# A recommender with two recurrent layers: the order of work between the first layer and the second

## The chip, the cores and the metric

The kernel runs on one core of one Trainium2 chip. The metric is the time on the device of one execution, in microseconds (us); lower is better. Three runs of the kernel before took 2012.16, 2012.26 and 2012.96 us, median 2012.26.

## What is computed

The reference handles 1024 users, each with a history of 100 items of 128 features, and gives one score for each. A GRU runs over the history and gives `keys`; a small attention network scores every key against the item; the weighted sum of the keys is `pooled`. A second recurrent layer (AUGRU) runs over the same keys with an update gate that is scaled by a number for each step and user, taken from `pooled.T`. Its state at the end of the user's own history goes into a last small network.

```python
def gru_step(h, x_t):
    gi = x_t @ gru_Wih.T + gru_bih
    gh = h @ gru_Whh.T + gru_bhh
    ...
    h_new = (1.0 - z) * n + z * h
...
score = _mlp(feat, [(att_W0, att_b0), (att_W1, att_b1), (att_W2, att_b2)], jax.nn.relu)
attn = jax.nn.softmax(score, axis=1)[..., 0]
pooled = jnp.einsum('bt,btd->bd', attn, keys)
att_seq = pooled.T[:T]

def augru_step(h, inp):
    x_t, a_t = inp
    ...
    u = a_t[:, None] * u
    h_new = (1.0 - u) * h + u * h_hat
```

The second layer can't begin before `pooled` is complete, since the number of its step t is feature t of `pooled`. The softmax over the history has to be complete for that.

## The kernel before, in words

Data lie with features on the 128 partitions and users along the free axis, in two halves of 512 users (`Half`, `HB`). Instructions stand in each engine's queue in the order in which the program issues them (`tc.manual_schedule`), and each engine has one queue. The program has two parts.

**The GRU part** (`gru_phase`, L201) loops over 100 steps and both halves; a step is packed matmuls of 32 output columns each. Beside it run the attention network (`attend`, L714), the softmax in blocks (`softmax`, L790), the weighted sums on POOL and DVE (`Half.pool`, L630) and the store of every four keys to memory (`Half.store`, L620: 1 MB for each half, on SP's DMA queue). After the last step, L956 to L1062, come the tail of the attention network, the last block of the softmax and the rest of the sums. In that tail:

- `half.store((T - 1) // G)` at L1021 puts the last keys of both halves in SP's queue.
- `gather_early(n)` (L887) issues the next n gathers of key rows (`load_row`, L183, the DMA at L190) from POOL. They bring keys 4 to 11 of half 0, sorted by length of history, 16 rows in all; 13 are issued in the GRU part, the rest at L1464.
- POOL forms the first 16 columns of each 32-column block of the sums for half 0, DVE for half 1 (L1043 to L1045). L1047 stores the first 16 features: half 1 by SP's queue, half 0 by ACT's.
- `half.pool(T, nc.vector, rest)` at L1054 leaves DVE with the other columns, reading the softmax weights from PSUM. The multiply is L652, the add L653.

**The branch** (L1533). A number worked out from the lengths, `over`, is loaded into a register of each engine. It selects one of three copies of the AUGRU part, written out for other widths: each step handles only the users whose history is still running, sorted by length. The copy for the usual widths is `augru(0)`; with these inputs it is the one that runs. In the program's text it stands last, in the Else part of the outer test.

**The AUGRU part** (`augru_phase`, L1064) gathers the stored weights in sorted order (`gather_weights`, L1094, four DMAs from POOL at L155 for each half), then issues the remaining row gathers, then opens the three gates of step 1 of both halves with the part of the matmuls that needs keys alone (`open_gates`, L1182, matmul at L1187). `EARLY_BANKS` and `LATE_BANKS` say which PSUM banks these six take; the banks were used by the GRU part. `first_state` (L1119) turns column 0 of the gathered weights into a row with four matmuls against an identity (L1111) and multiplies it into the state of step 0, on DVE (L1122, L1123). Then come the steps:

- `half_step(t, i)` (L1202) closes the gates with the state (`close_gate`, L1189, matmul at L1191), lets ACT apply the sigmoids and DVE do the rest, and opens the gates of the half's next step. Both halves alternate.
- `load_key(t, i)` (L1156) brings the key of step t. For keys 0 to 3 it transposes four 128x128 tiles on TensorE (L1170) into the one bank of the pool `pa` and ACT copies it out (L1171); for later keys DVE transposes 32x32 blocks. Keys 2 and 3 are loaded within steps 1 and 2.
- `first_weights`, `store_weights` and `load_att` bring the numbers of step 1, and those of later steps through memory.
- From step `one` on both halves go together (`whole_step`, L1273).
- `predict(0, last=True)` (L1324) computes the last scores; DVE adds them to the earlier ones in `all_y` (L1414), which `earlier_results` loads at L1438, and SP stores the 1024 scores (L1415), the last instruction of the copy.

After the branch all engines meet in a closing barrier.

Of the kernel before, what the change touches and what calls it, by code (L numbers as in the profile page):

```python
# [9 lines left out]
F32 = mybir.dt.float32  # L10
# [9 lines left out]
P = 128  # L20
B = 1024
T = 100
HB = 512
NH = B // HB
# [3 lines left out]
R = 32  # L28
KH = HB // R
# [22 lines left out]
G = 4  # L52
# [3 lines left out]
FIRST = [sum(READ[:q]) for q in range(len(READ))]  # L56
# [23 lines left out]
BQ = B // (P // R)  # L80
# [4 lines left out]
def kernel(ctx: ExitStack, tc: tile.TileContext, a: dict, out: bass.AP):  # L85
# [26 lines left out]
    nc = tc.nc  # L112
# [25 lines left out]
    item = const.tile([P, B], F32, name="item")  # L138
    hist = const.tile([P, B], F32, name="hist")
    pooled = const.tile([P, NK, R], F32, name="pooled")  # L140
    idx = const.tile([P, GH, NH * 3], I32, name="idx")
    idx_k = const.tile([P, KH, NH], I32, name="idx_k")
    used_s = const.tile([P, NH, GH, SOON], U8, name="used_s")
# [2 lines left out]
    h3 = [h_all[:, i, :] for i in range(NH)]  # L146
# [4 lines left out]
    later = {}  # L151
# [49 lines left out]
    def gru_phase(pools):  # L201
# [32 lines left out]
        wp = pools.enter_context(tc.tile_pool(name="wp", bufs=2))  # L234
# [7 lines left out]
        for _ in range(2):  # L242
            p = pa.tile([P, HB], F32, tag="a", name="pd")
# [465 lines left out]
        halves = [Half(i) for i in range(NH)]  # L709
# [177 lines left out]
        def gather_early(n):  # L887
            for _ in range(n):
                next(more_early)
# [3 lines left out]
        for s in range(T):  # L893
            last = s == T - 1
            n, due = divmod(s - again, 4)
            n, i = divmod(n, NH)
# [120 lines left out]
        some(6, 7)  # L1017
        for half in halves:
            key(1, half)
        for half in halves:  # L1020
            half.store((T - 1) // G)  # L1021
        stage(2)
        exponents()
        for half in halves:
            gates = (item[:, half.cols], s_bs[NH * ((soft["j"] - 1) % 2) + half.i])
            later["gates", half.i] = gates
            for to, (n, f) in zip(gates, (("u", AF.Sigmoid), ("h", AF.Tanh))):
                if half.i:
                    p = banks["f"].pop(0)
                else:  # L1030
                    p = pa.tile([P, HB], F32, tag="a", name=f"p{n}")
                nc.tensor.matmul(
                    p,
                    lhsT=later["w" + n][:, 1, :],
                    rhs=later["key", 0, half.i],
                    start=True,
                    stop=True,
# [5 lines left out]
        halves[0].product(soon)  # L1043
        halves[0].pool(T, nc.gpsimd, soon)
        halves[1].pool(T, nc.vector, soon)  # L1045
        gather_early(3)
        for half, eng in zip(reversed(halves), (nc.sync, nc.scalar)):  # L1047
            eng.dma_start(
                out=pooled_d[0][half.cols, :].rearrange("(k r) c -> r k c", r=R),
                in_=pooled[:R, half.ks, soon],  # L1050
            )
        for half in reversed(halves):
            half.todo = late[half.i]
            half.pool(T, nc.vector, rest)  # L1054
            t = blocked(s_bs[NH * (soft["j"] % 2) + half.i])
            nc.vector.tensor_mul(t, later["used"][:, half.ks, :], pooled[:, half.ks, :])
            to = pooled_d[1][half.cols, :].rearrange("(k r) f -> r k f", r=R)
            later["att", half.i] = [(to[:, :, : R - SOON], t[:R, :, rest])]
            later["att", half.i] += [
                (to[:, :, p * R - SOON : (p + 1) * R - SOON], t[p * R : (p + 1) * R])  # L1060
                for p in range(1, P // R)
            ]  # L1062

    def augru_phase(pools, widths, alive):  # L1064
# [4 lines left out]
        wp = pools.enter_context(tc.tile_pool(name="wp3", bufs=3))  # L1069
# [11 lines left out]
        wr, wu, wh = later["wr"], later["wu"], later["wh"]  # L1081
# [5 lines left out]
        def bank(name, n=None):  # L1087

            if n is None:
                n = ring.pop(0)  # L1090
                ring.append(n)
            return ps[n].tile([P, HB], F32, tag="g", name=name)
# [26 lines left out]
        def first_state(i, p):  # L1119
            weight_row(0, i, p)  # L1120
            u, h = gates[i]
            nc.vector.tensor_mul(p, p, u)  # L1122
            nc.vector.tensor_mul(h3[i], p, h)  # L1123
            r = sorted_rows[i][:, :, 1:SOON]
            nc.vector.tensor_mul(r, r, used_s[:, i, :, 1:])
# [30 lines left out]
        def load_key(t, i):  # L1156

            q = max(j for j, first in enumerate(FIRST) if first <= t)
            w, m, r = widths[t], t - FIRST[q], rows[q, i]
            if t >= one and i:  # L1160
                k = keys.pop((t, 0))
            else:
                k = qp.tile([P, HB], F32, name="k3")
            keys[t, i] = k
            if t >= one:
                k = k[:, ts(i, P)]
            if q < WHOLE:
                p = pa.tile([P, HB], F32, tag="a", name="pk3")
                for g in range(-(-w // P)):
                    nc.tensor.transpose(p[:, ts(g, P)], r[:, g, ts(m, P)], ident)  # L1170
                nc.scalar.copy(k[:, :w], p[:, :w])  # L1171
            else:
                w, n = -(-w // R), KH // len(r)
                for j, part in enumerate(r):
                    u = min(w - j * n, n)
                    if u > 0:
                        nc.vector.transpose(
                            k.rearrange("p (k r) -> p k r", r=R)[:, j * n : j * n + u, :],
                            part[:, :u, ts(m, R)],
                        )  # L1180
# [21 lines left out]
        def half_step(t, i):  # L1202


            w, h = widths[t], h3[i][:, : widths[t]]
            before, after = ((t - 1, 1), (t, 1)) if i == 0 else ((t, 0), (t + 1, 0))
            if before in resets:
                open_state(*before)
            pr = close_gate(t, i, "pr", wr, h)
            pu = close_gate(t, i, "pu", wu, h)  # L1210
            nc.scalar.activation(pr, pr, AF.Sigmoid, bias=later["br"])
            nc.scalar.activation(pu, pu, AF.Sigmoid, bias=later["bu"])
            state = states.pop(1 - i, None)
            if state is not None:
                nc.vector.tensor_mul(state[0], state[0], state[1])  # L1215
            r = wp.tile([P, HB], F32, name="r3")[:, :w]
            nc.vector.tensor_mul(r, h, pr)
            if state is not None:
                nc.vector.tensor_sub(state[3], state[0], state[2])
            if t == 1:  # L1220
                first_weights(i, spare)
                load_key(2, i)
            nc.vector.tensor_mul(pu, pu, att.pop((t, i))[:, :w])
            rest = wp.tile([P, HB], F32, name="rest")[:, :w]

            nc.vector.scalar_tensor_tensor(  # L1226
                out=rest, in0=pu, scalar=1.0, in1=h, op0=ALU.subtract, op1=ALU.mult
            )
            later["pace"] = rest[:, 0:1]
            resets[t, i] = r, pu, rest  # L1230
            if after[0] < min(T, one) and (*after, "pr") not in opened:
                open_gates(*after)
            elif after[0] == one < T:
                open_both(one, "pr", "pu", "ph")
            if t == 1 and i:
                store_weights(1, spare)
                load_key(3, 0)
            elif t == 1:
                open_state(1, 0)
                store_weights(0, pa.tile([P, HB], F32, tag="a", name="pw"))  # L1240
                first_state(1, spare)
            elif t == 2 and i == 0:
                load_key(3, 1)
            if t + 2 < T:
                load_att(t + 2, i)

            if t == FIRST[1] - 1:
                load_key(t + 1, i)
            if FIRST[1] - 2 < t < T - 2:
                load_key(t + 2, i)  # L1250
# [73 lines left out]
        def predict(g, last=False):  # L1324
# [80 lines left out]
            for q in range(P // R):  # L1405
# [4 lines left out]
                    start=True,  # L1410
                    stop=True,
                )
            all_y = later["all_y"]
            nc.vector.tensor_add(all_y, p, all_y)  # L1414
            nc.sync.dma_start(  # L1415
                out=out.rearrange("(q c) -> q c", c=BQ),
                in_=all_y.rearrange("(q r) c -> q r c", r=R)[:, 0, :],
            )

        def last_places():  # L1420
            own = sp.tile([P, 1], F32, name="own3", bufs=1)
# [12 lines left out]
                later["places"].append(row)  # L1434

        def earlier_results():
            later["all_y"] = wp.tile([P, BQ], F32, tag="att_t", name="all_y", bufs=2)
            nc.sync.dma_start(  # L1438
                out=later["all_y"],
                in_=early_d.rearrange("(q c) o -> q (o c)", c=BQ)  # L1440
                .unsqueeze(1)
                .to_broadcast([P // R, R, BQ]),
            )
# [17 lines left out]
        gates = [later["gates", i] for i in range(NH)]  # L1461
        keys.update({(1, i): later["key", 1, i] for i in range(NH)})
        sorted_rows = [gather_weights(i) for i in range(NH)]
        for k in range(13, KH):  # L1464
            load_row(1, 0, k)
        open_gates(1, 1, EARLY_BANKS)
        open_gates(1, 0, LATE_BANKS)
        spare = bank("spare", EARLY_BANKS[-1])
        first_state(0, pa.tile([P, HB], F32, tag="a", name="first"))
        ahead = load_rows(1, 1, widths[FIRST[1]], kp)  # L1470
        due = spread_over(-(-widths[FIRST[1]] // R), NH * (FIRST[1] - 2))
# [57 lines left out]
    def augru(n):  # L1529
        with ExitStack() as pools, tc.manual_schedule():  # L1530
            augru_phase(pools, WIDTHS[n], ALIVE[n])

    over = nc.values_load(over_d, min_val=0, max_val=len(LINES))  # L1533
    with tc.If(over > 0) as many:
        with tc.If(over < 2) as fits:
            augru(1)
        with fits.Else():
            augru(2)
    with many.Else():
        augru(0)  # L1540


# [64 lines left out]
```

## Time and profile before

| what | value |
|---|---|
| median of 3 runs | 2012.26 us |
| the profiled execution | 2012.06 us |
| its span in the profile | 2010.3 us |
| TensorE (PE) busy | 1987.7 us, 99% |
| VectorE (DVE) busy | 1673.9 us, 83% |
| GpSimd (POOL) busy | 1273.8 us, 63% |
| ScalarE (ACT) busy | 936.0 us, 47% |
| last GRU-part matmul ends | 1405.51 us |
| first AUGRU-part matmul starts | 1410.66 us |
| last store issued (L1415) | 2007.65 us |
| DMA traffic | 204.88 MB, mean 102 GB/s |

The profile is of one execution. Its times count from the start of the span; the execution's own time has some 1.8 us more around the span. Lines such as L652 are lines of the kernel before. A line of the timeline gives start, length, engine, line, operation, the tiles written and read, and in brackets how long the engine had been idle and who ended that. A line of the chain of work that ended last gives start, length and engine or DMA. PEld is TensorE's weight load. SPq and ACTq are the DMA issues of SP and ACT. In a table of stretches each engine has its busy time in us and its number of instructions; then come the granted clock of TensorE as a share of full speed, the busy share of the DMA engines and GB/s.

### The profile page before, as it was taken

The numbers are of one execution on the slowest core, as the hardware profiler recorded it, in microseconds if no ns is written. First come the engines' busy times: TensorE is split into PE (matmuls) and PEld (weight loads), VectorE is DVE, ScalarE is ACT, GpSimd is POOL, SyncE is SP. The second block draws the span as 40 slices with busy tenths as digits, with TensorE's granted clock in tenths as the row PEclk, the third lists the DMA queues.
The fourth block names the chain that finished last, engine by engine and source line by source line (L and its number), as shares of the span: only waits on it lengthen the run. The fifth ranks groups of instructions, "written<-read, shape, count | busy, mean of one in ns | idle before, by whom it ended". The sixth has DMA issues, their size and how long they took to land.

```text
span 2010.3 us, 40989 instructions
## 1 busy us (share of the span) xinstructions
PE 1987.7 (99%) x15348; PEld 1198.2 (60%) x15348; DVE 1673.9 (83%) x3033; ACT 936.0 (47%) x1681; POOL 1273.8 (63%) x1325
## 2 busy tenths in 40 slices
PE   9999999999999999999999999999899999999998
PEld 2346666666555555555555555545444556678997
DVE  7888999887978887888878888998577778888985
ACT  4445454454444454444444454455243444455553
POOL 0333939669796959495887868898674454445331
PEclk9999999999999999999999999999899999999998
DMA  4443333323334434333333333332543333343331
GB/s 124 98 117 92 107 104 102 94 82 104 115 113 103 118 108 123 115 109 105 106 101 99 107 98 101 107 95 76 138 126 103 96 110 97 94 103 95 85 80 28
DMA packets 243152, 204.88 MB, mean 102 GB/s; under 512 B 60582, under 2 KB 205966, under 8 KB 242942
## 3 DMA queue, kind: packets, MB, share of 16 engines
q1 hardware_dynamic: 229646, 169.55, 30.4%
q0 software_dynamic: 12480, 32.05, 5.8%
q8 instruction: 123, 2.02, 0.4%
q14 instruction: 87, 0.71, 0.1%
q10 hardware_dynamic: 816, 0.56, 0.1%
HBM read 146.03 MB, written 54.41 MB: 100 GB/s over the span
## 4 chain that ended last, share of the span: by engine, by line
PE 96%; DVE 1%; DMA 1%; issue 0%; ACT 0%; POOL 0%; SPq 0%; DVEq 0%; POOLq 0%; ACTq 0%
PE ps L547 51%; PE pm L723 18%; PE ph L1191 4%; PE pr L1191 4%; PE pu L1191 4%; PE pu L1187 4%; PE ph L1187 4%; PE pr L1187 4%; DMA rows<-keys_d,idx_k 1%; PE last L690 1%; PE pr L1269 0%; DMA item<-in_item 0%; PE ph L1269 0%; PE p L1389 0%; DVE pu L1215 0%
## 5 line engine op out<-in xcount | busy, mean ns | idle before, releaser
L547 PE MATMUL ps<-x,wih 128*32 128x512 f32 x4800 | 712.5, 593 | 0.0
L547 PE MATMUL ps<-hn,whh 128*32 128x512 f32 x4752 | 705.9, 592 | 1.3 <-ACT hn L595 1.3
L547 PEld LDWEIGHTS ps<-x,wih 128*32 128x32 f32 x4800 | 301.9, 110 | 225.7 <-issue 39.7
L547 PEld LDWEIGHTS ps<-hn,whh 128*32 128x32 f32 x4752 | 299.5, 110 | 222.5 <-issue 35.5
L559 ACT ACTIVATE r<-ps,brz 128x512 f32<-128x512 f32 x200 | 137.5, 688 | 382.6 <-PE ps L547 382.4
L532 POOL TENSOR_TENSOR xm<-x,m 128x512 f32<-128x512 f32 x200 | 234.9, 1175 | 68.2 <-DMA m<-mask_d 67.9
L533 POOL TENSOR_TENSOR hist<-hist,xm 128x512 f32<-128x512 f32 x200 | 258.2, 1291 | 15.7
L190 POOL DMA_INDIRECT rows<-keys_d,idx_k x218 | 212.5, 975 | 82.2 <-POOL rows L189 45.9
L653 POOL TENSOR_TENSOR pooled<-pooled,kw 128x512 f32<-128x512 f32 (+1 forms) x190 | 243.7, 1283 | 14.9
L652 POOL TENSOR_TENSOR kw<-kt,e 128x512 f32<-128x512 f32 (+1 forms) x190 | 205.6, 1082 | 67.9 <-DVE e L841 67.9
L723 PE MATMUL pm<-hn,wk 128*32 128x512 f32 x1200 | 245.5, 592 | 0.6 <-issue 0.6
L723 PE MATMUL pm<-kq,wkq 128*32 128x512 f32 x1200 | 245.5, 592 | 0.0
L578 ACT ACTIVATE ps<-ps,bih 128x512 f32<-128x512 f32 x200 | 132.4, 662 | 224.8 <-DVE ps L577 223.8
L567 DVE SCALAR_TENSOR_TENSOR u<-ps,bhh,r 128x512 f32<-128x512 f32 x198 | 147.5, 745 | 70.6 <-PE ps L547 68.1
L1199 ACT ACTIVATE c<-ph,bh 128x510 f32<-128x510 f32 (+57 forms) x174 | 88.1, 506 | 251.0 <-PE ph L1191 203.3
L723 PE MATMUL pm<-mv,w 128*32 128x512 f32 (+1 forms) x808 | 194.9, 592 | 0.0
L582 DVE TENSOR_TENSOR d<-hn,ps 128x512 f32<-128x512 f32 x198 | 136.1, 687 | 35.9 <-ACT ps L578 35.2
L583 DVE TENSOR_TENSOR d<-ps,d 128x512 f32<-128x512 f32 x200 | 138.4, 692 | 29.1 <-ACT ps L579 13.3
L595 ACT COPY hn<-ps 128x512 f32<-128x512 f32 x200 | 116.4, 582 | 94.3 <-DVE kq L589 92.6
L189 POOL COPY rows<-rest 128x1 f32<-128x1 f32 x202 | 38.0, 188 | 192.6 <-DVE rest L1226 186.5
L577 DVE TENSOR_TENSOR ps<-ps,u 128x512 f32<-128x512 f32 x200 | 140.0, 700 | 20.8
L584 DVE TENSOR_TENSOR ps<-ps,d 128x512 f32<-128x512 f32 x200 | 139.9, 699 | 6.8
(255 smaller groups left out, 3141.0 us busy)
## 6 DMA issues: line engine op xcount, KB each, us to landing
x<-in_hist_x SPq DMA_DIRECT2D x210, 256.0 KB
keys_d<-kt SPq DMA_DIRECT2D x48, 1024.0 KB
m<-mask_d SPq DMA_DIRECT2D x200, 128.0 KB
rows<-keys_d,idx_k POOLq DMA_INDIRECT x218
s_b<-mv SPq DMA_DIRECT2D x200, 8.0 KB
keys_d<-kt SPq DMA_DIRECT2D x32, 64.0 KB
mask_i<-in_mask SPq DMA_DIRECT2D x8, 200.0 KB
part_d<-part SPq DMA_DIRECT2D x2, 400.0 KB
```

The costliest lines, as they stand in the source:

```text
L190: nc.gpsimd.indirect_dma_start(out=r[:, at, :], out_offset=None, in_=keys_d[q], in_offset=bass.IndirectOffsetOnAxis(ap=idx_k[:, k, i : i + ...
L532: nc.gpsimd.tensor_mul(d, x, m)
L533: nc.gpsimd.tensor_add(acc, acc, d)
L547: nc.tensor.matmul(p[ts(q, R), :], lhsT=w[:, g, ts(q, R)], rhs=v, start=(j == 0), stop=(j == len(parts) - 1),)
L567: nc.vector.scalar_tensor_tensor(out=u, in0=ph, scalar=bhh[:, 2:3], in1=r, op0=ALU.add, op1=ALU.mult,)
L577: nc.vector.tensor_add(pi, pi, u)
L584: nc.vector.tensor_add(pi, pi, d)
L652: eng.tensor_mul(d, k, w)
L653: eng.tensor_add(acc, acc, d)
L723: nc.tensor.matmul(p[i][s, :], lhsT=w[:, s], rhs=v, start=start, stop=stop)
L1187: nc.tensor.matmul(p, lhsT=m[:, 1, :], rhs=k, start=True, stop=False)
L1191: nc.tensor.matmul(p, lhsT=m[:, 0, :], rhs=v, start=False, stop=True)
```

## The change

- The test of the branch is turned round: `augru(0)` is now the first body, and the other two stand behind it.
- The store of the scores moves from the end of the copies to behind the branch. `all_y` is no tile of the AUGRU part any more but lies in the memory of `pooled`.
- `load_key` for steps 2 and 3, both halves, moves from steps 1 and 2 to between the opening matmuls and `first_state`. Three matmuls into the bank `spare` are added behind them; nothing reads their result.
- The store of the last keys moves behind the store of the pooled sums.
- One row gather moves from the GRU part to behind the gathers of the weights.

```diff
@@ tile_rec_kernel
     pooled = const.tile([P, NK, R], F32, name="pooled")
+    all_y = pooled.rearrange("p k r -> p (k r)")[:, :BQ]
@@ gru_phase, after the last step
         for half in halves:
             key(1, half)
-        for half in halves:
-            half.store((T - 1) // G)
         stage(2)
...
         halves[0].pool(T, nc.gpsimd, soon)
         halves[1].pool(T, nc.vector, soon)
-        gather_early(3)
+        gather_early(2)
         for half, eng in zip(reversed(halves), (nc.sync, nc.scalar)):
             eng.dma_start(
                 out=pooled_d[0][half.cols, :].rearrange("(k r) c -> r k c", r=R),
                 in_=pooled[:R, half.ks, soon],
             )
+        for half in halves:
+            half.store((T - 1) // G)
@@ half_step
             if t == 1:
                 first_weights(i, spare)
-                load_key(2, i)
...
             if t == 1 and i:
                 store_weights(1, spare)
-                load_key(3, 0)
             elif t == 1:
                 open_state(1, 0)
                 store_weights(0, pa.tile([P, HB], F32, tag="a", name="pw"))
                 first_state(1, spare)
-            elif t == 2 and i == 0:
-                load_key(3, 1)
@@ predict and earlier_results
-            all_y = later["all_y"]
             nc.vector.tensor_add(all_y, p, all_y)
-            nc.sync.dma_start(
-                out=out.rearrange("(q c) -> q c", c=BQ),
-                in_=all_y.rearrange("(q r) c -> q r c", r=R)[:, 0, :],
-            )
...
-            later["all_y"] = wp.tile([P, BQ], F32, tag="att_t", name="all_y", bufs=2)
             nc.sync.dma_start(
-                out=later["all_y"],
+                out=all_y,
@@ augru_phase
-        for k in range(13, KH):
+        for k in range(12, KH):
             load_row(1, 0, k)
         open_gates(1, 1, EARLY_BANKS)
         open_gates(1, 0, LATE_BANKS)
         spare = bank("spare", EARLY_BANKS[-1])
+        for t in range(2, FIRST[1]):
+            for i in range(NH):
+                load_key(t, i)
+        for _ in range(3):
+            nc.tensor.matmul(spare, lhsT=wr[:, 1, :], rhs=h3[0], start=True, stop=True)
         first_state(0, pa.tile([P, HB], F32, tag="a", name="first"))
@@ tile_rec_kernel, at the end
     over = nc.values_load(over_d, min_val=0, max_val=len(LINES))
-    with tc.If(over > 0) as many:
+    with tc.If(over < 1) as fits:
+        augru(0)
+    with fits.Else():
         with tc.If(over < 2) as fits:
             augru(1)
         with fits.Else():
             augru(2)
-    with many.Else():
-        augru(0)
+    nc.sync.dma_start(
+        out=out.rearrange("(q c) -> q c", c=BQ),
+        in_=all_y.rearrange("(q r) c -> q r c", r=R)[:, 0, :],
+    )
```

## The prediction

> **What bounds the kernel now.** I read the busy shares first, then the chain of work that ended last, then the timeline around the one place where that chain leaves TensorE, then TensorE's granted clock there.
>
> ```profile
> PE 1987.7 (99%) x15348; PEld 1198.2 (60%) x15348; DVE 1673.9 (83%) x3033; ACT 936.0 (47%) x1681; POOL 1273.8 (63%) x1325
> ```
>
> TensorE is busy 99% of the span, so an edit elsewhere pays only where TensorE waits or runs at half clock. The chain shows the exception, the passage from the GRU to the AUGRU (start, length, what):
>
> ```profile
> 1406.92 0.73 POOL pooled L637
> ...
> 1407.80 11.85 DMA rows<-keys_d,idx_k
> 1419.64 2.09 DMA att_r<-pooled_d,idx
> 1424.01 2.07 PE pr L1191 x2
> ```
>
> For 17 us the chain runs over POOL and DMA: pooled sums, their store, the gathers of attention weights, the first state. The timeline names the actors:
>
> ```profile
> 1404.49 1.02 PE L1032 MATMUL last<-h_all,wh 128*128 128x512 f32 x2
> 1410.66 2.04 PE L1187 MATMUL pr<-hist,wr 128*128 128x510 f32 x2 [5.15 <-DVE last L652]
> 1410.35 0.96 POOL L190 DMA_INDIRECT rows<-keys_d,idx_k  x1 [0.31 <-issue]
> 1415.87 0.95 POOL L155 DMA_INDIRECT att_r<-pooled_d,idx  x1 [4.57 <-DMA pooled_d<-pooled]
> 1401.51 3.15 SPq L622 DMA_DIRECT2D keys_d<-kt  x2
> 1406.75 3.54 SPq L1048 DMA_DIRECT2D pooled_d<-pooled  x1
> 1412.82 0.43 DVE L652 TENSOR_TENSOR last<-kt,last 128x256 f32<-128x256 f32 x1
> 1440.97 1.02 PE L1191 MATMUL ph<-r,wh 128*128 128x510 f32 x2
> 1446.51 1.01 PE L1191 MATMUL ph<-r,wh 128*128 128x506 f32 x2
> ```
>
> TensorE stands still from 1405.51 to 1410.66, POOL from 1411.31 to 1415.87, each while it loads the branch value and jumps. The 32 KB pooled store of half 1 takes 3.54 us to issue on SP behind 2 MB of keys; its twin on ACT's queue takes 0.34. The last two lines are the points from which every half step is TensorE's six matmuls of 0.85 us. The stretches below end in TensorE's granted clock, DMA share and GB/s:
>
> ```profile
> 1406.29:1409.71 3.42, 0.00 (x0) 0.00 (x0) 3.24 (x9) 0.00 (x0) 2.89 (x4) 1.00 1.05 308
> 1413.12:1416.53 3.41, 3.41 (x5) 1.35 (x4) 1.24 (x3) 0.00 (x0) 0.66 (x1) 0.50 0.13 30
> 1419.95:1423.36 3.41, 1.30 (x6) 0.73 (x6) 0.80 (x2) 0.00 (x0) 2.54 (x3) 1.00 0.08 7
> 1426.77:1430.19 3.42, 3.42 (x15) 2.91 (x14) 0.74 (x2) 1.31 (x3) 2.02 (x3) 0.50 0.30 86
> 1996.79:2000.20 3.41, 3.41 (x18) 3.41 (x17) 1.11 (x5) 0.90 (x4) 0.49 (x1) 0.50 0.03 7
> ```
>
> After an idle stretch of 3.41 us (first line), and after one with little work (third), the clock is half for the next 6.8 us: 1409.7 to 1416.5 and 1423.4 to 1430.2. A matmul pair then takes 1.7 us instead of 0.85.
>
> **What the skill says.** The Trainium skill, "TensorE: Matmul & The Clock Gate", Part 1, has the clock at half or full, decided by a free-running activity window of about 3.4 us; the trace agrees (0.50 or 1.00, 6.8 us each time, edges on multiples of 3.41 us from the span's start). "Runtime: NRT & Kernel Launch", section Instruction fetch mechanics: fetching ahead is sequential, and a taken branch outside the window waits for a fetch of the target; the trace agrees in that TensorE's 16 KB instruction packet falls between 1408.0 and 1410.7, inside its idle time. The same page's launch section gives about 1.3 us for a register load from HBM, and "Advanced Engine Details and Errata", Control Flow Timing, about 108 ns for compare-and-branch. No row of this trace shows either alone.
>
> **The change part by part.**
>
> *Branch order.* Augru(0) now follows the test. What is left of the 5.15 us is load and compare: by the skill an estimate of 1.3 + 0.1 us, at most the 5.15 seen. I take 1.4 to 2.4, so TensorE is back at 1406.9 to 1407.9, before the clock falls at 1409.7. It then runs five of the six opening matmuls (5 x 0.85) until 1411.2 to 1412.2. The sixth, pu of half 0, reuses the PSUM bank of exponents that DVE reads last in L652 at 1412.82 to 1413.25. So it streams at 1413.4 and ends at 1414.27, however early TensorE came. Before, it ended near 1418.4.
>
> *Keys 2 and 3 moved in front.* Four load_key calls, each 4 transposes and an ACT copy, share one PSUM bank and so alternate. By the row pair at 1437.0 (transposes 0.60 with drain, 0.08, copy 0.59, two handovers of 0.17 together) one takes 1.44 us. The fourth starts at 1414.27 + 3 x 1.44 = 1418.6 and leaves TensorE at 1419.0. ACT has nothing else then. Their four spots in steps 1 and 2 are freed, 0.44 us of TensorE each at full clock. They issue no DMA.
>
> *Three filler matmuls.* 3 x 0.85 = 2.55, until 1421.6. Their bank was last read by DVE L653, ending 1413.7: no wait. They delay first_state only if the weights are there sooner. What they buy is work in the clock windows: in the before's own grid the windows from 1413.1 and 1416.5 hold 0.85 + 2 x 0.43 = 1.7 us and 2 x 0.43 + 0.9 = 1.8 us of streaming, some 50%. The low side in the trace: the window from 1419.95 (1.30 busy) lost the clock.
>
> *Stores and the gathers.* Pooled sums of half 1 are ready at 1406.72, of half 0 at 1407.65; issued unobstructed (0.34) and landed in about 2 us (the att_r gather took 2.09) they are there by 1410. The two key stores are now behind them on SP, about 9 us of DMA from 1408.6 to 1417.6 instead of 1402.9 to 1411.9; nothing but their own late gather wants them, SP issues nothing else until 1432.74. One row gather fewer stands in POOL's queue (0.95 + 0.30): POOL ends its two at 1410.04, loads and tests (1.4 to 2.7) and starts att_r at 1411.5 to 1412.8 instead of 1415.87. The fourth of them, 3 x 1.255 later, lands 2.1 us on if undisturbed, 5.3 if held up like the row gather issued at 1401.66 beneath the keys: 1417.3 to 1421.9. TensorE comes at 1421.6. So this gain is mostly covered by the longer queue on TensorE. The row gather moved behind the eight att_r ones costs POOL 1.26 at 1421 to 1427, where its next due work waits for a rest tile from 1429 on: nothing.
>
> *First state.* Weights 8 x 0.107 from 1421.6, drain, two DVE multiplies (0.70, 0.69, as at 1422.53): half 0's step 1 starts at 1424.1. Before: 1424.01. No gain up to here.
>
> *Steps 1 and 2 at full clock.* Half 1's step 1 gives the full-clock template: from its pr at 1434.41, r is done 2.54 later, the weight row's copy 3.48, rest 4.94. Half 0's step 1 adds three DVE operations (0.68, 0.70, 0.69, gaps 0.03) before half 1 can start: 7.15 us against 10.40 (1424.01 to 1434.41). Half 1's step 1 (to the ph at 1440.97, 6.56) loses two transposes: 5.66. Step 2 of half 0 (5.54) loses one: 5.10. Sum: 3.25 + 0.90 + 0.44 = 4.59, less the 0.1 of the start: 4.5 us. All later half steps are the same 5.06 us, POOL's row gathers are paced by them, so the lead is kept.
>
> *End.* The store leaves SP behind the same DVE add (2007.61). SP's own jump out of the branch has from 1999.1 to 2007.6. DVE must jump over two unused bodies before the closing barrier; at 0.1 to 3.7 us (5.15 less the load) against the store's 2.7 to landing, that costs 0 to 1.0; I take 0.2. The output buffer's new place costs nothing, pooled being idle by then. The clock's fall at 1996.8 comes some 1 us later in the work when that is 4.5 us ahead: 0.2 back. Were a window nearer the start caught with too little work, 1.2 lost.
>
> Sum: the profiled execution's 2012.06 (span 2010.3 and 1.8 around it) less 4.5 is 2007.6. The median of the runs is 0.2 above the profiled one: 2007.8. A change under 0.2%, 4.0 us, can't be told from none here: the limit is 2008.2.
>
> **Rivals.** *The clock drops in the wait for the sixth matmul* (chance 0.09). Place: the window 1409.7 to 1413.1. If TensorE is back before about 1406.7, its five matmuls end by 1411.0 and that window holds under 1.3 us of work, 38%. Windows of the last steps lost the clock near 36% and kept it near 40% by my count of streamed columns. At half clock pu ends at 1415.1, the key loads take 1.87 each, the fillers 1.7 each, and they end at 1426.7: step 1 starts at 1429.2, 5.2 late, and the 4.6 saved is more than gone: 2012.9, slower than before. For it: the load's 1.3 us. Against: the idle time seen is 5.15.
>
> *Transposes don't count as activity* (0.10): the clock falls at 1416.5, the fillers run at half clock, step 1 starts 2.6 late: 2010.3. Nothing in this trace has transposes alone in a window.
>
> *The branch doesn't get cheaper* (0.05): TensorE is back at 1410.66, the gates end at 1418.4, keys and fillers at 1425.7, step 1 at 1428.2: 0.4 gained, 2011.8.
>
> *The gathers starve behind the key stores* (0.05): landing after 1426 instead of by 1421.9 eats all 4.5, and the idle clock adds 3: from 2012 to beyond 2016.3. Against: 7 us of delay on top of a normal 2.1 was seen nowhere.
>
> *Everything as forecast and the last steps keep full clock longer* (0.07): 1 to 2 us more, 2006.3.
>
> The forecast has 0.64, within 2006.6 to 2008.8. Left out of 2005.8 to 2010.6 are the clock drop, the dear branch and the starved gathers, 0.19. Faster by over 0.2%: some 0.85 of 0.64, and 0.07: 0.61. Slower by over 0.2%: 0.05. Within: 0.34.
>
> **What would show it.** TensorE's first L1187 near 1407; the sixth beginning at 1413.4; transposes of L1170 at 1414 to 1419; att_r from about 1412; clock 1.00 throughout 1405 to 1440; L1191's first pr near 1424, half 1's 7.2 later. A 0.50 in any window before 1430, or a first pr after 1426, makes the forecast wrong; a first pr before 1422.5 means the fillers or the wait for DVE were not on the path.

## The result, and the profile after

The changed kernel is **slower**, by three thousandths: 2018.12 us median against 2012.16 us of the kernel before measured beside it, ratio 1.0031 (95% interval 1.0023 to 1.0039). The forecast was a gain, to 2007.8 us, with a range of 2005.8 to 2010.6; the result is a loss and lies outside it. The profiled execution took 2018.99 us (span 2017.1). Line numbers below are those of the changed kernel, one above the old ones where the old ones are quoted (L653 and L654 are the old L652 and L653).

The timeline of the changed kernel (start, length, engine, line, tiles; in brackets the idle time before and who ended it), at the place that the prediction shows of before:

```profile
1406.71 0.34 SPq L1047 DMA_DIRECT2D pooled_d<-pooled  x1
1407.10 2.18 SPq L623 DMA_DIRECT2D keys_d<-kt  x2
1407.65 0.38 ACTq L1047 DMA_DIRECT2D pooled_d<-pooled  x1
...
1413.81 2.04 PE L1188 MATMUL pr<-hist,wr 128*128 128x510 f32 x2 [8.33 <-DVE pooled L654]
1415.37 0.95 POOL L156 DMA_INDIRECT att_r<-pooled_d,idx  x1 [5.35 <-DVE s_b L1057]
...
1420.82 0.60 PE L1171 MATMUL pk<-ident,rows 128*128 128x128 f32 x4
...
1425.32 2.74 PE L1464 MATMUL spare<-h_all,wr 128*128 128x512 f32 x6
...
1427.89 1.05 PE L1112 MATMUL first<-ident,att_r 128*128 128x128 f32 x8
...
1432.60 0.70 DVE L1123 TENSOR_TENSOR first<-first,item 128x512 f32<-128x512 f32 x1 [18.15 <-remote]
...
1434.08 2.07 PE L1192 MATMUL pr<-h_all,wr 128*128 128x510 f32 x2 [5.13 <-DVE h_all L1124]
```

TensorE came back at 1413.81, not at 1407: 8.33 us idle where it had been 5.15. What ended the wait is the last multiply-and-add of DVE in the GRU part (L654). POOL's first weight gather came after the DVE operation behind that (L1057). The keys and fillers then hold TensorE until the weight row at 1427.89, and DVE takes up the weight row 3.66 us after its last matmul, at 1432.60, with nothing seen between. Step 1 starts at 1434.08 instead of 1424.01.

The branch itself did become free. These lines give instructions of TensorE's sequencer (ns, smallest/median/largest, and the starts). First come the load of the branch value and the branch in the kernel before, then the branch in the changed one:

```profile
L1533 PEldq TENSOR_LOAD <-over_d x1: 688/688/688, 1402.3 to 1402.3; - x1
...
L1534 PEldq COMPARE_BRANCH  x1: 7392/7392/7392, 1403.1 to 1403.1; - x1
```

```profile
L1530 PEldq COMPARE_BRANCH  x2: 92/1989/3886, 1403.1 to 2012.0; - x2
```

7.39 us became 0.09. The second branch of the changed kernel, 3.89 us at 2012.0, is the new jump over the two other bodies at the end.

The clock, in stretches on the changed kernel's own grid (busy time and count of PE, PEld, DVE, ACT, POOL, then granted clock, DMA share, GB/s):

```profile
1407.22:1410.63 3.41, 0.00 (x0) 0.00 (x0) 3.17 (x9) 0.00 (x0) 2.35 (x3) 1.00 0.80 204
1410.63:1414.05 3.42, 0.24 (x1) 0.27 (x2) 3.18 (x8) 0.00 (x0) 0.00 (x0) 0.50 0.98 257
...
1427.70:1431.11 3.41, 1.25 (x9) 0.86 (x7) 0.00 (x0) 0.00 (x0) 1.91 (x2) 1.00 0.35 91
1431.11:1434.53 3.42, 0.45 (x1) 0.45 (x2) 1.52 (x3) 0.00 (x0) 0.00 (x0) 0.50 0.06 24
```

After each of the two long waits the clock is half, from 1410.6 to 1417.5 and from 1431.1 to 1437.9, so steps 1 and 2 again run at half clock for a part.

Times from the end of the last GRU matmul (1405.51 before, 1405.48 after) set the passage side by side with the forecast:

| point | before | forecast | after |
|---|---|---|---|
| first opening matmul | 5.15 | 1.4 to 2.4 | 8.33 |
| POOL's first weight gather | 10.36 | 6.0 to 7.3 | 9.89 |
| sixth opening matmul starts | 12.42 | 7.9 | 14.49 |
| weight row done | 16.88 | 17.0 | 23.47 |
| DVE's first-state multiply | 17.01 | 17.1 | 27.13 |
| step 1 of half 0 | 18.49 | 18.6 | 28.61 |
| candidate of step 3, half 1 (`c<-ph`, the sixth) | 57.14 | 52.6 | 64.35 |
| from DVE's last add to the end of the span | 2.65 | 2.9 | 3.55 |

The lag behind the kernel before is 7.17 us from step 3 to about 1840 us. In the last 160 us it shrinks to 5.96, and the last line of the table adds 0.90: the span is 6.86 us longer.

### The profile page after: what moved, and what is told of

Same layout as the page of the kernel before. It is cut to its first block, busy times and chain, and to the rows that moved or that the text cites. A ratio compares the mean times of both kernels' runs of the same rounds, so it can differ in the third digit from the quotient of the medians.

```text
span 2017.1 us, 41023 instructions
## 1 busy us (share of the span) xinstructions
PE 1985.4 (98%) x15354; PEld 1079.7 (54%) x15354; DVE 1673.7 (83%) x3033; ACT 936.4 (46%) x1681; POOL 1275.5 (63%) x1325
## 4 chain that ended last, share of the span: by engine, by line
PE 95%; DVE 2%; another core or an unknown queue 1%; issue 1%; ACT 0%; DMA 0%; SPq 0%; DVEq 0%; ACTq 0%
PE ps L548 50%; PE pm L724 17%; PE ph L1192 4%; PE pr L1192 4%; PE pu L1192 4%; PE ph L1188 4%; PE pr L1188 4%; PE pu L1188 4%; PE last L691 1%; PE pr L1266 0%; PE ph L1266 0%; DMA item<-in_item 0%; PE p L1386 0%; DMA bm<-in_b 0%
## 5 line engine op out<-in xcount | busy, mean ns | idle before, releaser
L548 PE MATMUL ps<-x,wih 128*32 128x512 f32 x4800 | 769.2, 592 | 0.0
L548 PE MATMUL ps<-hn,whh 128*32 128x512 f32 x4752 | 763.6, 592 | 2.1 <-ACT hn L596 2.1
L548 PEld LDWEIGHTS ps<-x,wih 128*32 128x32 f32 x4800 | 283.2, 110 | 268.4 <-issue 245.9
L548 PEld LDWEIGHTS ps<-hn,whh 128*32 128x32 f32 x4752 | 280.9, 110 | 267.4 <-issue 242.5
L724 PE MATMUL pm<-hn,wk 128*32 128x512 f32 x1200 | 256.6, 592 | 0.9 <-issue 0.9
L724 PE MATMUL pm<-kq,wkq 128*32 128x512 f32 x1200 | 256.6, 592 | 0.0
L654 POOL TENSOR_TENSOR pooled<-pooled,kw 128x512 f32<-128x512 f32 (+1 forms) x190 | 244.0, 1284 | 14.9
L653 POOL TENSOR_TENSOR kw<-kt,e 128x512 f32<-128x512 f32 (+1 forms) x190 | 205.8, 1083 | 67.9 <-DVE e L842 67.8
```

Source lines behind the costliest of these rows:

```text
L548: nc.tensor.matmul(p[ts(q, R), :], lhsT=w[:, g, ts(q, R)], rhs=v, start=(j == 0), stop=(j == len(parts) - 1),)
L653: eng.tensor_mul(d, k, w)
L654: eng.tensor_add(acc, acc, d)
L724: nc.tensor.matmul(p[i][s, :], lhsT=w[:, s], rhs=v, start=start, stop=stop)
```

## The experiments

The theories. **A, coarse waits:** the body that stands first in the text gets one lump of waits. The semaphores that each instruction waits for show it: its first opening matmul waits for TensorE's own last GRU matmul, DVE's last L654 and ACT's last activation, and the other five for nothing; in the body that stands last, the first waits for an early DVE operation and the sixth alone for a late one. **B, the longer queue:** keys and fillers ahead of the first state delay it. **C:** TensorE's time in the branch of before was the fetch of the code that it jumps to, queued behind 2 MB of key stores. **D:** a pooled store behind a key store lands late. The rivals on record (starved gathers, clock) stand beside them.

The runs were made on four chips, and the kernel before is not equally fast on them (2007.2 us on the first, 2010.1, 2010.7 and 2010.1 on the others), so ratios are to the runs of before on the same chip. The points are again counted from the last GRU matmul; "late" is the time between the last weight-row matmul and DVE's multiply, and "step 3" is the candidate of step 3, half 1.

| run | chip | ratio (95%) | first matmul | weight gather | late | step 1 | step 3 |
|---|---|---|---|---|---|---|---|
| x1_last_body | 1 | 0.9974 (0.9963 to 0.9985) | 1.49 | 10.21 | 0.14 | 18.46 | 52.31 |
| x2_no_fillers | 1 | 1.0014 (1.0008 to 1.0021) | 8.33 | 9.89 | 0.14 | 24.58 | 60.06 |
| x3_first_body_alone | 1 | 1.0002 (0.9993 to 1.001) | 8.33 | 9.89 | 0.13 | 18.12 | 55.10 |
| x4_stores_alone | 1 | 0.9994 (0.9986 to 1.0002) | 1.73 | 10.52 | 0.14 | 19.07 | 56.71 |
| x5_changed_again | 2 | 1.0045 (1.003 to 1.006) | 8.33 | 9.89 | 3.48 | 28.41 | 64.25 |
| x6_keys_on_act_queue | 2 | 1.001 (1.0003 to 1.0017) | 1.49 | 6.35 | 0.15 | 24.83 | 60.36 |
| x7_act_queue_no_fillers | 2 | 1.0009 (1.0 to 1.0017) | 1.74 | 6.67 | 0.14 | 22.68 | 59.14 |
| x8_fillers_ahead | 2 | 1.0055 (1.0039 to 1.007) | 8.33 | 9.89 | 0.28 | 28.51 | 64.07 |
| x9_both_pooled_on_sp | 3 | 0.9986 (0.9979 to 0.9994) | 1.75 | 6.59 | 0.38 | 18.70 | 56.12 |
| x11_fillers_no_keys | 3 | 1.0018 (1.0011 to 1.0025) | 8.33 | 9.90 | 0.14 | 21.84 | 61.77 |
| x12_keys_fillers_alone | 3 | 1.0007 (0.9999 to 1.0016) | 4.98 | 10.46 | 1.17 | 23.99 | 59.51 |
| x13_changed_beside | 4 | 1.0031 (1.0019 to 1.0043) | 8.33 | 9.89 | 3.60 | 28.47 | 64.20 |
| x14_last_body_beside | 4 | 1.0009 (1.0003 to 1.0016) | 1.68 | 9.86 | 0.14 | 18.46 | 58.80 |
| x15_short_fillers_beside | 4 | 0.999 (0.9983 to 0.9997) | 1.47 | 6.54 | 1.92 | 18.73 | 56.23 |
| x16_before_beside | 4 | before itself | 5.14 | 10.27 | 0.14 | 18.86 | 57.67 |

The short-filler kernel also ran on chip 3 (x10_short_fillers): 0.9989 (0.9983 to 0.9996), late by 3.30.

**The body's place, put back in the changed kernel.**

```diff
-    with tc.If(over < 1) as fits:
-        augru(0)
-    with fits.Else():
+    with tc.If(over > 0) as many:
         ...
+    with many.Else():
+        augru(0)
```

> The changed kernel with its usual body back in the last place of the text; all its other edits stay. Theory A (coarse waits): the body that stands first in the text waits once, at its first matmul, for the last DVE multiply of the GRU part, and at POOL's first weight gather for the last DVE operation; in the last place each bank has its own wait. Then the first opening matmul no longer waits for L654 (1413.66) and the time falls to 2007.8 to 2011.8: 2007.8 if theory C holds too (the 5.15 us of TensorE's branch before were the fetch of the far body, queued behind 2 MB of key stores that now come later, so TensorE is back by 1407.5), 2011.8 if the fetch takes as long as before (back at 1410.7). Theory B (TensorE's longer queue ahead of the first state, no matter where the body stands): TensorE starts sooner but the first state stays late, 2014 to 2017. If position doesn't matter at all: 2018.

Measured: 0.9974, faster than before. The timeline of this run:

```profile
1405.75 1.09 PE L1188 MATMUL pr<-hist,wr 128*128 128x510 f32 x2 [1.49 <-DVE pooled L654]
...
1412.04 1.12 PE L1188 MATMUL pu<-hist,wu 128*128 128x510 f32 x2 [1.78 <-DVE last L653]
...
1414.47 0.95 POOL L156 DMA_INDIRECT att_r<-pooled_d,idx  x1 [5.68 <-DMA rows<-keys_d,idx_k]
...
1420.05 1.05 PE L1112 MATMUL first<-ident,att_r 128*128 128x128 f32 x8
...
1421.24 0.70 DVE L1123 TENSOR_TENSOR first<-first,item 128x512 f32<-128x512 f32 x1 [8.00 <-PE first L1112]
...
1422.72 1.12 PE L1192 MATMUL pr<-h_all,wr 128*128 128x510 f32 x2 [1.61 <-DVE h_all L1124]
```

TensorE is back 1.49 us after the GRU part, as soon as its branch ends (1401.83 to 1405.58), and of the six matmuls only the last is held up by DVE. The clock stays full through the whole passage. But for POOL's gather (10.21, forecast 6.0 to 7.3) this is the forecast's passage, made by the old branch order: step 1 at 18.46 (forecast 18.6), step 3 at 52.31 (52.6).

**The body's place alone, in the kernel before:** the same edit the other way round.

> The kernel before with the test turned round and nothing else: the usual body stands first in the text. Theory A: the first opening matmul waits for the last DVE multiply, 1413.3 to 1413.9 instead of 1410.66, the six end near 1420.8, POOL's first weight gather comes at 1414.5 to 1415.9, step 1 at 1424 to 1425; with some 0.9 us for the jump over the other bodies at the end, 2012.5 to 2014. Forecast on record (the branch itself is what held TensorE): first matmul by 1408, full clock in steps 1 and 2, 2008 to 2010.

```profile
1413.21 2.04 PE L1187 MATMUL pr<-hist,wr 128*128 128x510 f32 x2 [8.33 <-DVE pooled L653]
...
1423.00 1.79 PE L1191 MATMUL pr<-h_all,wr 128*128 128x510 f32 x2 [1.62 <-DVE h_all L1123]
```

Theory A again, to the hundredth: 8.33 us. But alone it costs nothing that can be measured (1.0002). The gathers, not TensorE, set step 1 there: the six matmuls end just before the fourth gather lands. Step 3 even comes at 55.10, where the kernel before has 57.1 to 57.7 on other chips, and the end takes that back. The end costs more than theory A said: 4.99 us from the last add to the end of the span against 2.66 in x1 and x4. SP issues its store, branches at 2002.46, and its next instruction comes at 2005.16. The changed kernel and its variants with the body first, with the store behind the branch, pay 3.35 to 3.59; that part of the change does save some 1.4 of the jump's 2.3.

**The stores alone, in the kernel before** (the hunks in the GRU part and the row gather).

> The kernel before with the key store behind the pooled store (and the one row gather moved), branch order, keys and output store as before. Theory C (TensorE's branch waits for its fetch behind the key stores): first opening matmul at 1406 to 1407.5 instead of 1410.66. If the fetch isn't held up by them: 1410.7 again. In both cases POOL's first weight gather moves from 1415.87 to 1411.5 to 1412.5, the fourth lands near 1417.5, and step 1 starts at 1420 to 1421 instead of 1424.0: 2008 to 2010. If the gathers starve behind the key stores (the rival on record): step 1 at 1424 or later, 2012 or more.

```profile
L1534 PEldq COMPARE_BRANCH  x1: 3885/3885/3885, 1401.4 to 1401.4; - x1
```

Theory C holds: with the usual body still last, TensorE's branch takes 3.89 us instead of 7.39. A 16 KB instruction packet starts 1.2 us into the branch (1402.57), in the kernel before 5.0 us into it (1408.1). Of the 3.89 us, 2.3 run beside the last matmuls, since the value is loaded before they end, so TensorE is back at 1.73. That POOL's gather would come by 1412.5 did not hold: it stays at 1414.26, 10.52 after the GRU part, since half 0's pooled store lands only at 1413.0. TensorE then waits for gathers with nothing to do, the clock is half from 1414.0 to 1427.7, and the time hardly moves (0.9994).

**Keys and fillers.** The three fillers taken out of the changed kernel:

> The changed kernel without the three filler matmuls. Theory B: they stand ahead of the first state in TensorE's queue, so its step 1 starts at least their 2.6 us sooner than 1434.08; time 2015.5. If the 3.6 us between the last weight-row matmul (1428.95) and DVE's multiply (1432.60) hang on them too, step 1 starts near 1428 and the time is about 2012. Theory A alone (all comes from the late start of TensorE and POOL, the fillers are covered by the gathers): within 0.5 of 2018, since the fourth gather has landed at 1421.2 anyway.

Ratio 1.0014, some 1.7 to 3 thousandths better than with them, but on another chip. The line of the weight row, first here and then in x3, on the same chip:

```profile
1427.02 1.13 PE L1112 MATMUL first<-ident,att_r 128*128 128x128 f32 x8 [0.71 <-ACT k L1172]
```

```profile
1420.04 1.34 PE L1111 MATMUL first<-ident,att_r 128*128 128x128 f32 x8
```

In both runs TensorE is back at 8.33 and the first gather comes at 9.89, and neither has the gap of the next section. With the keys in front the weight row is done at 22.96, without them at 16.50; 1.3 us of that is half clock that lasted longer. So theory B holds for the keys where TensorE is late. For the fillers it is not shown here: with them the weight row is done at 23.47, only 0.5 later, and the rest of the 4.0 us by which step 1 comes sooner is that gap. Only the moved keys and fillers, in the kernel before:

> The kernel before with keys 2 and 3 and the three fillers ahead of the first state, and nothing else: branch order, stores and gathers as before. TensorE returns at 1410.7 and runs the six at half clock until 1418.4; keys end near 1423.5, fillers near 1426.2, later than the gathers (1421.7): step 1 starts at 1428 to 1429 instead of 1424.0, then steps 1 and 2 at full clock give 4.6 back. Ratio 0.9995 to 1.0005. If the clock falls all the same: 1.002.

1.0007, not told from no change. The weight row is done at 21.34 instead of 16.88 (or 17.24 in x16), and steps 1 and 2 give half of it back: step 3 is at 59.51 against 57.1 to 57.7. DVE's multiply was 1.17 late here. So the same keys and fillers cost with TensorE back at 8.33, do little at 5, and pay at 1.5, where they fill a wait for gathers that is there anyway (x1 against x4, on one chip: step 3 at 52.31 and 56.71).

**The 3.66 us.** First the changed kernel again, then the fillers put ahead of the keys, then the keys back in the steps with the fillers kept.

> The changed kernel itself once more. In its first profile DVE's multiply of the first state starts 3.6 us after the last weight-row matmul (1428.95 to 1432.60) with nothing seen between. If that belongs to the kernel, the gap is there again, and step 1 starts some 10 us later than in the kernel before; ratio 1.003 again. If it was one execution's accident, DVE follows within 0.2 us and step 1 starts 3.5 us sooner.

> The changed kernel with the three fillers ahead of the keys instead of behind them; same instructions, same count. If the 3.6 us before DVE's multiply come from the six semaphore waits that stand between the fillers and the weight row in the first body, they go: DVE follows the last weight-row matmul within 0.2 us and step 1 starts 3 to 3.6 us sooner (time 3 us less than the changed kernel). If they come from the number or place of the instructions, the gap stays.

> The changed kernel (usual body first) with keys 2 and 3 back in steps 1 and 2, the three fillers kept. Opening matmuls end near 1420.8, fillers near 1423.4, the weight row follows at once. If the late signals of TensorE in the first body come from long matmuls standing beside its list of semaphore waits, DVE's multiply again comes 1.5 to 3.5 us after the last weight-row matmul. If they need the keys, it follows within 0.2 us. Time by theory B: 1.5 to 3 us less than the changed kernel.

The gap came back (3.48). With the fillers ahead it moved: ACT took up the fourth key 1.2 us late, and the time didn't improve. Without the keys it was gone there, and came later, in step 1 (bunched signals from 1430.9 to 1431.1); the ratio is 1.0018. The trace records when TensorE raises its semaphore, the signal for which the other engines wait. In the first profile of the changed kernel its matmuls end at 1428.06 (fillers) and 1428.28 to 1428.95 (weight row), and the signals come at

```
1430.26  1430.99  1432.40  1432.44  1432.48
```

so they are late, and then bunched 0.04 us apart. The theory of the six waits falls: signals bunched like this appear in every kernel's profile on chips 2, 3 and 4, and in those of the result, and behind 1400 us in none on chip 1. The profiles of chip 1 hold 2237 to 2241 signals of some 2240 due; the others hold 2051 to 2090. Records are missing, then, on the very chips where signals come late, so the recording itself may have a part in it; no run here tells. To tell the change from the chip, four kernels were run side by side:

> The changed kernel, on one chip with the next three. If the 3.5 us before DVE's first multiply belong to late signals of TensorE on some chips, then on a chip whose records show none of them the multiply follows the weight row within 0.2 us, step 1 starts 6 to 7 us later than in the kernel before, and the ratio is 1.001 to 1.002. If they belong to the kernel, the gap is there on every chip and the ratio is 1.003 to 1.0045.

> The usual-body-last kernel again, beside the others. Quiet chip: ratio 0.9974 again, the difference to the changed kernel 0.0035 to 0.005 (coarse waits and nothing else). Chip with late signals: its own gap between weight row and multiply anywhere from 0 to 3.5 us, ratio 0.997 to 1.0.

> The short-filler kernel again. Its step 1 could start at 1420.5 but for the 3.3 us by which the multiply came late in its first profile. Quiet chip: ratio 0.9955 to 0.9965, below the usual-body-last kernel. Chip with late signals: 0.9985 to 0.9995 again.

> The kernel before itself, for its profile on this chip. Quiet chip: no bunched signals of TensorE near 1881 to 1950, span near 2005. Chip with late signals: they are there, span 2008 to 2012.

This chip was not a quiet one either. The kernel before has late signals too (x16):

```profile
1428.12 1.02 PE L1191 MATMUL ph<-r,wh 128*128 128x510 f32 x2
...
1430.39 0.58 ACT L1171 COPY k<-pk 128x506 f32<-128x506 f32 x1 [1.93 <-PE ph L1191]
```

ACT was free from 1428.48, and the four transposes that it copies had ended by 1428.28; TensorE's signals come at 1428.28 and then only at 1430.37. The usual-body-last kernel, whose step 1 starts at 18.46 here as well, meets them one step later (x14):

```profile
1428.60 0.70 DVE L1223 TENSOR_TENSOR pu<-pu,at 128x510 f32<-128x510 f32 x1 [3.60 <-ACT at L1131]
```

TensorE idles for it and the clock is half from 1428.7 to 1438.9; the gain is gone: 1.0009 instead of 0.9974. Beside it on this chip the changed kernel is at 1.0031. So late signals struck the changed kernel on its path in all three profiles, for 3.3 to 3.5 us (the gaps of 3.48 to 3.66 less the 0.14 of the other kernels); whether they would be absent on chip 1 was not seen, since the changed kernel didn't run there. Its twin without fillers did, and there, with no late signal in the passage, it is slower than before (1.0014).

**The pooled store.** Half 0's leaves ACT's queue 0.55 us behind the first 1 MB key store. In the changed kernel it lands, by its semaphore, at 1413.6, 6.0 us after its issue; half 1's, ahead of the keys, after 1.7 us. The key stores put on ACT's queue, behind both:

```diff
-            half.store((T - 1) // G)
+            half.store((T - 1) // G, nc.scalar)
```

> The changed kernel with the usual body last (as in the run of that name) and the two key stores issued from ACT's queue, so that they stand behind both pooled stores and not between them. Theory D (half 0's pooled store, issued 0.55 us after the first 1 MB key store, lands only when that has drained, 6.8 us later, and POOL's gathers wait for it): it now lands near 1408.5 and POOL's first weight gather starts at 1409 to 1410.5 instead of 1414.47. TensorE's keys and fillers still end at 1420.05, so step 1 stays at 1422.5 to 1423 and the ratio near 0.997. If D is wrong, POOL's gather stays at 1414 to 1414.5.

> As the run with the key stores on ACT's queue, without the three fillers. Theory D: the gathers have landed by 1416 to 1418, so nothing but the keys stands ahead of the first state: step 1 starts 2.0 to 2.6 us sooner, 1420.1 to 1420.7, and the ratio falls to 0.9955 to 0.9965, if the clock stays full. If the gathers still land at 1420.5, TensorE waits for them with the clock at half afterwards, and the ratio is 0.999 to 1.001.

```profile
1410.90 0.95 POOL L156 DMA_INDIRECT att_r<-pooled_d,idx  x1 [1.81 <-DMA rows<-keys_d,idx_k]
...
1416.72 0.58 ACT L1172 COPY k<-pk 128x506 f32<-128x506 f32 x1 [11.45 <-issue]
```

Theory D holds: both pooled stores land by 1409.2 and the gather starts 6.35 after the GRU part instead of 10.21. But ACT now issues for 3.4 us, comes to its branch at 1411.25, and copies the first key at 1416.72, 2.8 us after the transposes, with nothing seen to wait for. That its code is fetched behind the keys is likely, but not shown: an instruction packet comes at 1415.1, and the trace does not say for which engine. TensorE waits, the clock falls at 1416.2, and neither kernel reaches the ratio expected. Both pooled stores on SP instead:

```diff
-        for half, eng in zip(reversed(halves), (nc.sync, nc.scalar)):
+        for half, eng in zip(reversed(halves), (nc.sync, nc.sync)):
```

> The changed kernel with the usual body last and both pooled stores on SP, half 0's behind half 1's, so that the key stores on SP stand behind both and ACT's queue stays free. Theory D (a pooled store behind a 1 MB key store lands 5 to 7 us late): both land by 1409.5, POOL's first weight gather starts near 1410.9 as with the key stores on ACT's queue, and ACT's own code arrives in time (first key copy at 1414, not 1416.7). Keys and fillers still hold TensorE until 1420: step 1 at 1422.5 to 1423, ratio 0.997 to 0.998.

```profile
1404.89 1.26 SPq L1047 DMA_DIRECT2D pooled_d<-pooled  x2
...
1410.24 0.95 POOL L156 DMA_INDIRECT att_r<-pooled_d,idx  x1 [2.04 <-DMA rows<-keys_d,idx_k]
...
1413.09 0.58 ACT L1172 COPY k<-pk 128x506 f32<-128x506 f32 x1 [8.71 <-PE pk L1171]
```

The gather, ACT's copy and step 1 come as expected; the ratio is 0.9986 where 0.997 to 0.998 was. The early gathers now wait behind the key stores in their turn: the first lands at 1415.2, 4.9 us after its issue, where the first of x3 took 2.4. In step 1 signals come bunched at 1427.2 to 1427.4, the clock is half from 1431.0 to 1434.5, and step 3 is at 56.12, not at 52.31 as in x1. The last run puts one filler of 256 columns behind each key, in TensorE's wait for the copy, instead of three whole ones at the end:

> As the run with both pooled stores on SP, but instead of the three whole fillers one of 256 columns behind each key, in the 0.7 us in which TensorE waits for ACT's copy. Theory D: the weights are there by 1417, TensorE has 0.87 us of work in each 1.33 us and keeps the clock, and step 1 starts 2 to 2.5 us sooner than with whole fillers, at 1420.2 to 1421; ratio 0.995 to 0.9965. If the clock falls (0.50 in a stretch before 1435), 0.998 to 1.0.

The weight row is done 1.5 us sooner than with whole fillers (15.33 against 16.84), and DVE's multiply, late by 1.9 and 3.3 us, ate it. On two chips this kernel is faster than before by a thousandth (0.9989 and 0.9990), as is x9 (0.9986). No kernel was found that beats the kernel before by more than that on a chip with late signals; on the quiet chip x1 gains 2.6 thousandths.

## Why the prediction was wrong

**The step that failed** is the first: "TensorE is back at 1406.9 to 1407.9, before the clock falls" and "then runs five of the six opening matmuls". I took the waits of `augru(0)` for fixed, as the trace of before shows them, each bank with its own. They belong to its place in the text. Moved to the front, the first matmul waits for the last DVE multiply: 1413.81, later than before. Runs show it both ways: 8.33 us with the body first, in every one of them, and 1.47 to 1.85 with it last and the stores moved. Everything behind it on TensorE stood in a queue that was sized for a start at 1407. So step 1 began 10.1 us later than in the kernel before: 6.6 us of that is there when the weight row is done, and 3.5 is the gap behind it.

**The branch's price** was misread as well, though that did no harm. I took the 5.15 us for load and jump, and said that no row of the trace shows either alone. The lines of L1533 and L1534 do: the load takes 0.69 us from 1402.3 and the branch 7.39 from 1403.1, both begun before the last matmul ends at 1405.51. The estimate of 1.3 us came from the Trainium skill, "Runtime: NRT & Kernel Launch", The launch sequence, which gives it for the register loads before a kernel; one value took half of that here. The rest was a fetch behind the key stores. What that page says in Instruction fetch mechanics of a taken branch, that it waits for a fetch of its target where that lies outside the window, agrees with 7.39 us before, 3.89 with the stores moved and 0.09 without a jump. Moving the stores was enough; turning the branch round was not needed.

POOL's 4.57 us were misread the same way: its load (1407.5) and its branch (1408.3, 0.05 us) were over, and it waited for half 1's pooled sums, which landed at 1415.06.

**Stores and gathers.** "Landed by 1410" failed for half 0: 1413.6 (theory D). POOL's first weight gather, forecast 1411.5 to 1412.8, came at 1415.37, behind DVE's last operation. The fourth gather's landing, forecast 1417.3 to 1421.9, was 1421.2, in the range by luck: the gathers were issued 2.6 to 3.9 us too late and then landed undisturbed, 2.0 us after the fourth's issue. The starving that the rival priced hit the small store ahead of the gathers.

**Keys and fillers** were sized rightly: 1.33 us a key (forecast 1.44), 2.57 for the fillers (2.55). What failed is that they were "mostly covered" by the gathers. With the late start they end at 1427.9, 6.7 us behind the fourth landing.

**The first state** began 3.66 us after its weight row instead of at once; late signals of TensorE were in no rival, though those of the kernel before are in its trace too.

**Steps 1 and 2** were right in mechanism and size: forecast 4.59 us, and x1 needs 33.85 us from step 1 to step 3 where before needed 38.65, so 4.8 (on two chips). The changed kernel got 2.9 of it (35.74), since the clock was half from 1431.1 to 1437.9.

**The end** was given 0.2 of a bound of 0 to 1.0; it took 0.9 (3.55 against 2.65). The engine was the right one: DVE branches at 2013.17, its next instruction comes at 2016.24, and after that one the closing barrier goes on.

**The rivals.** The clock did fall, by the wait for DVE, but for another reason than the one priced (an early TensorE that runs dry). That transposes don't count for the clock is refuted: in x2 the stretch from 1422.85 to 1426.26 holds 1.92 us of key transposes and no other matmul, and the clock stays full in the next stretch. I gave slower by over 0.2% a chance of 0.05: a rival in which the turned branch brings later waits was missing.

## What to carry to other kernels

Where a body of code stands can change its waits, so before an engine is said to be free by a moved block, look at what the block's first instructions on each engine wait for in the new place. Before a jump is blamed, see what the fetch of its target queues behind; moving a bulk store can be cheaper than moving the code. Work put into a wait is worth something only as long as the wait is there: the same keys and fillers gained with TensorE back at 1.5 us, on the quiet chip, and lost with it back at 8.3.

## What was not expected of the hardware

A 32 KB store issued half a microsecond behind a 1 MB store, on another queue, landed 6.0 to 7.1 us after its issue (the changed kernel and x4), against 1.7 to 3.6 ahead of it (the changed kernel and x9). On three chips TensorE's signals come up to 3.5 us late and then bunched 0.04 us apart, in every kernel; on a fourth no signal of this passage was late in any of the four kernels run there. Behind step 3 the lag between two kernels of one chip can stay the same to 0.01 us for 380 us (5.48 us, x13 behind x16), but from step 3 to the last candidate the quiet chip needs 533.8 to 535.9 us and the others 537.0 to 540.2, whatever the kernel. What makes the signals late, and why the first body gets its waits in one lump, is open; neither was tried apart.
